# Gates of a graph network in pairs: half of the nodes as a difference on top of the other half's sums, and four relation products beside the gates

## The chip, the cores and the metric

The kernel runs on one core of a Trainium2 chip, as one launch. It is measured in device microseconds from the start to the end of an execution; the time before is the median of three runs, 1405.69 us (1404.71 to 1413.34). Five engines work side by side, each through its own queue in order: TensorE (PE, with its weight loads as PEld), VectorE (DVE), ScalarE (ACT), GpSimd (POOL) and SyncE (SP), which here only issues DMAs. They wait for each other by semaphores.

## The reference

The whole program is a stack of four graph layers, each followed by a feed-forward layer, on 256 nodes of 768 features. The change is in the first graph layer alone. It computes two rounds of this (x is 256 x 768; a batch of 8 graphs has 32 nodes each; 64 query vectors per graph):

```python
def _rgcn(x, W_rel, W_root, bias, src, dst, etype):
    xr = jnp.einsum('ni,rio->rno', x, W_rel)          # 3 relations
    msg = xr[etype, src]
    out = x @ W_root + bias
    for r in range(NUM_RELATIONS):
        m = etype == r
        s = segment_sum(where(m[:, None], msg, 0.0), dst)
        c = segment_sum(m, dst)
        out = out + s / jnp.maximum(c, 1.0)[:, None]
    return out

def _gate(h, q, Wg, bg, Wq, bq):
    h3 = h.reshape(B, N, F)
    hg = jnp.einsum('bnf,gf->bng', h3, Wg[:, :F])
    qg = jnp.einsum('blf,gf->blg', q, Wg[:, F:]) + bg
    attn = jax.nn.sigmoid(hg[:, :, None, :] + qg[:, None, :, :])
    qi = jnp.einsum('bnlf,blf->bnf', attn, q)
    alpha = jax.nn.sigmoid(h3 @ Wq[:, :F].T + qi @ Wq[:, F:].T + bq)
    return alpha * jnp.tanh(qi) + (1.0 - alpha) * h3

h = relu(_rgcn(x, W_rel1, W_root1, b1, ...)); h = _gate(h, ...)
h = relu(_rgcn(h, W_rel2, W_root2, b2, ...)); h = _gate(h, ...)
```

The costly part is `attn`: for every graph, node, query and feature one sigmoid of a sum of a node's term (hg) and a query's term (qg), multiplied by q and summed over the queries.

## The kernel before

The nodes are held in two chunks of 128 (four graphs each), the features as six blocks of 128 on the partitions. A round ("layer" in the loop at the end of the code) has these stages.

*Relation products and RGCN.* `z_of` (L457 to L466) multiplies one chunk of nodes with half of one relation's weights: six matmuls of 128x384. There are 12 such products in a round (3 relations, 2 chunks, 2 halves). The RGCN then adds, for each feature block, the root product and the relation products spread over the edges (`ps_rgcn`, L102 and L728); ScalarE's Relu gives `gT`.

*Terms.* `q_terms` and `node_terms` compute qg and hg, six matmuls for a half. `split3` takes each result apart into three bf16 parts that add up to it (ScalarE and VectorE in turn, over seven steps), and DMAs place the parts on partitions: `ga` holds the first two parts of the query terms, `gb` the third part and, on partitions 64 to 111, the three parts of 16 node terms. `gb` has two copies, u = 0 and 1, one for each half of a graph's 32 nodes. Most node rows go through a DRAM tile (`hg_rows`).

*Gates.* A unit is one graph and one feature block: 48 units a round. `form` (L758 to L771) makes a unit in two steps, u = 0 and 1. In each, TensorE sums the terms of 16 nodes with all 64 queries into two PSUM banks by multiplying with matrices of ones and zeros (`sela`, `selb`): two matmuls of 128x512 for each bank, four in all. Then ScalarE takes the sigmoid of the two banks at once (L769). A round thus has 384 gate matmuls. The bank pairs (`acc2`) are two in number. Of every three units, two are multiplied by q on GpSimd (L789) and one on VectorE (L796, for which ScalarE first copies q to the PSUM bank `qy`, L786); VectorE sums all (L774, `total`) into `qiT`. Gate tiles come from five buffers (tag `z`), which the relation products' results use as well.

*Beside the gates.* After each step's matmuls, `next(beside)` issues one further matmul of a chain of generators: the remaining `q_terms` and `node_terms`, then for each chunk the two halves of alpha's product (`alpha_nodes` L632, `alpha_gates` L647, the latter waiting until its sums are five steps old), and the first chunk's `blend`. Their follow-up work is put down by `later(n, ...)` to be issued n steps on. `blend` copies alpha from PSUM, transposes it, takes the sigmoid and a tanh (into bank `qy`), and mixes the new features `nT` on VectorE, in three turns whose distance is `gap` steps.

*End of a round.* What is left of the chain is issued, then the second chunk's `blend`. In the first round its turns alternate with the 12 relation products for the second round (`more`), in the second round with nothing.

The order on the engines is that of the program for everything inside `pin`; the rest, DMAs among it, is put in order by the framework. Each engine works strictly in its own order. Weights come through a ring of eight buffers, and a load is issued by SyncE when the buffer it replaces has had its last reader; `parts` tiles (`stg`) are three.

## Time and profile before

| what | us |
|---|---|
| median of three runs | 1405.69 |
| the profiled execution | 1404.96 |
| its span, first to last instruction | 1403.2 |
| first round: gates on TensorE | 134.3 to 284.3 |
| first round: gates on VectorE (first to last sum) | 144.2 to 297.7 |
| first round: last alpha, blend, 12 relation products | 297.7 to 348.0 |
| second round: RGCN | 348.0 to 379.1 |
| second round: gates on TensorE | 390.7 to 538.2 |
| second round: gates on VectorE (first to last sum) | 400.8 to 550.4 |
| second round: last alpha, blend | 550.4 to 559.7 |

The rest of the program, before 94 us and after 560 us, is not touched. Times in the profile are those of one execution; "busy" is the time in which an engine's instructions run. Matmuls overlap, so that the duration of one (379 ns for 128x512) is longer than the distance from one to the next (217 ns): sums of work on TensorE are made with the distance. An f32 matmul of 128x384 appears as two records, together 0.65 us. The number in brackets behind a row of a time line is the engine's idle time before it, with what ended that time.

### The profile page before, as it was taken

How to read it: one execution, taken by the hardware profiler on the slowest of the kernel's cores; microseconds unless marked ns; L12 is line 12 of the kernel's file. 1: busy time of each engine (PE TensorE's matmuls, PEld its weight loads, DVE VectorE, ACT ScalarE, POOL GpSimd, SP SyncE). 2: the span in 40 equal slices, each digit the busy share in tenths (PEclk: the TensorE clock that was granted, in tenths of full speed). 3: DMA queues.
4: the chain of work that ended last, by engine and by line, in shares of the span. 5: the costliest groups of instructions: out<-in, count | busy, mean ns of one | idle time of the engine just before them, and what ended most of it. 6: DMA issues, size and time to landing. Idle time of an engine off the chain costs nothing. (4 is left out here: it accounts for less than half of the span.)

```text
span 1403.2 us, 13971 instructions
## 1 busy us (share of the span) xinstructions
PE 1246.0 (89%) x5088; PEld 765.4 (55%) x5088; DVE 671.2 (48%) x1278; ACT 476.0 (34%) x826; POOL 360.1 (26%) x200
## 2 busy tenths in 40 slices
PE   7999999969998884799899978987887999878998
PEld 4576444436843442575545554545575545467854
DVE  4330899950069998406446271067252101365033
ACT  1012777721177764115114212215221111173122
POOL 1000999920069995000111101021011000100000
PEclk9999999989999997799999979998989999975989
DMA  9332150314240021241573139942019799801000
GB/s 343 124 110 96 45 180 19 102 34 167 104 127 8 0 102 44 76 166 40 195 293 117 53 125 363 364 170 102 23 59 347 286 392 402 344 1 36 32 0 23
DMA packets 77450, 196.92 MB, mean 140 GB/s; under 512 B 8764, under 2 KB 23712, under 8 KB 77248
## 3 DMA queue, kind: packets, MB, share of 16 engines
q1 hardware_dynamic: 69088, 162.28, 32.3%
q0 software_dynamic: 6576, 28.95, 5.8%
q10 hardware_dynamic: 1712, 4.72, 0.9%
q8 instruction: 44, 0.72, 0.2%
q14 instruction: 30, 0.25, 0.1%
HBM read 177.61 MB, written 14.87 MB: 137 GB/s over the span
## 5 line engine op out<-in xcount | busy, mean ns | idle before, releaser
L789 POOL TENSOR_TENSOR gate<-gate,qT 128x2048 f32<-128x2048 f32 x64 | 287.8, 4522 | 241.7 <-ACT gate L769 241.3
L774 DVE TENSOR_REDUCE qiT<-gate 128x32 f32<-128x2048 f32 x96 | 215.0, 2279 | 16.2 <-POOL gate L789 15.2
L769 ACT ACTIVATE gate<-gate_acc,bg 128x1024 f32<-128x1024 f32 x192 | 209.6, 1113 | 38.2 <-PE gate_acc L765 35.5
L764 PE MATMUL gate_acc<-sela,ga 128*128 128x512 bf16 x384 | 147.3, 384 | 25.2 <-ACT gate L769 24.5
L765 PE MATMUL gate_acc<-selb,gb 112*128 112x512 bf16 x384 | 147.8, 385 | 0.0
L1159 PE MATMUL up_acc<-w_e,xgT 128*64 128x384 f32 (+1 forms) x432 | 96.4, 489 | 0.0
L765 PEld LDWEIGHTS <-gb 112*128 112x128 bf16 x384 | 37.6, 98 | 96.2 <-issue 71.4
L796 DVE TENSOR_TENSOR gate<-gate,ps_qy 128x2048 f32<-128x2048 f32 x32 | 72.9, 2277 | 0.2 <-ACT gate L769 0.2
L1159 PEld LDWEIGHTS up_acc<-w_e,xgT 128*64 128x64 f32 (+1 forms) x432 | 46.9, 154 | 44.6 <-issue 27.2
L764 PEld LDWEIGHTS <-ga 128*128 128x128 bf16 x384 | 37.8, 98 | 47.7 <-issue 2.2
L647 PE MATMUL ps_alpha<-w_qb,qiT 128*128 128x384 f32 x96 | 44.1, 553 | 19.8 <-DVE qiT L774 19.8
L571 DVE TENSOR_TENSOR ps_hg<-ps_hg,hg 128x384 f32<-128x384 f32 x8 | 4.5, 562 | 107.8 <-ACT hg L570 107.8
L267 DVE CUSTOM_DVE_ANT_0 gat_dot<-xl,row 128x128 f32<-128x128 f32 (+2 forms) x56 | 23.8, 424 | 51.3 <-ACT xl L1537 18.9
L462 PE MATMUL ps_z<-w_rel,xT 128*128 128x384 f32 x144 | 47.9, 486 | 0.0
L462 PE MATMUL ps_z<-w_rel,nT 128*128 128x384 f32 x144 | 47.5, 490 | 0.0
L1126 POOL DMA_INDIRECT yg<-ys,rows x8 | 7.6, 953 | 153.5 <-DMA w_qk<-in_L_ffn_W_qkvT 100.9
L466 ACT COPY z<-ps_z 128x384 f32<-128x384 f32 x24 | 11.5, 478 | 104.5 <-PE ps_z L462 104.5
L1689 DVE TENSOR_TENSOR h<-up_acc,h 128x768 f32<-128x768 f32 x6 | 5.7, 957 | 80.1 <-PE up_acc L1159 80.1
L102 PE MATMUL ps_e<-xT,w_s 128*128 128x256 f32 x144 | 36.2, 417 | 7.4 <-DVE heads L1568 7.4
L171 PE MATMUL ps_tr<-ident,xn 128*128 128x128 f32 x84 | 16.7, 363 | 28.9 <-DVE xn L160 14.0
L632 PE MATMUL ps_alpha<-w_qa,gT 128*128 128x384 f32 x96 | 40.0, 498 | 0.0
L1126 POOL DMA_INDIRECT xg<-table,slots x12 | 11.7, 977 | 105.2 <-PE ps_xg L1134 46.3
(446 smaller groups left out, 2187.8 us busy)
## 6 DMA issues: line engine op xcount, KB each, us to landing
w_e<-in_L_ffn_W SPq DMA_DIRECT2D x32, 1152.0 KB, 12.2
w_rel<-in_L_gnn_W_rel SPq DMA_DIRECT2D x12, 1152.0 KB, 8.7
wi<-in_L_ffn_WiT SPq DMA_DIRECT2D x8, 1152.0 KB, 12.0
wo<-in_L_ffn_WoT SPq DMA_DIRECT2D x8, 1152.0 KB, 12.7
w_down<-in_L_ffn_W SPq DMA_DIRECT2D x8, 1152.0 KB
w_s<-in_L_ffn_Ws SPq DMA_DIRECT2D x5, 1152.0 KB, 8.9
w_root<-in_L_gnn_W_root SPq DMA_DIRECT2D x4, 1152.0 KB, 5.4
w_ga<-in_L_gnn_WgAT SPq DMA_DIRECT2D x4, 1152.0 KB
```

The source lines that it names most:

```text
L102: mm = nc.tensor.matmul(ps, w(k, lo, lo + P), xT[:, k, :], start=start and k == 0, stop=stop and k == kcs - 1)
L267: pin(nc.vector.tensor_tensor_reduce(t, xl[:, c, h * C:(h + 1) * C], r[:, h * C:(h + 1) * C], 1.0, 0.0, OP.mult, OP.add, accum_out=a2[:, w ...
L462: mm = nc.tensor.matmul(ps, hT[:, k, c * P:(c + 1) * P], w(k, i * 384, (i + 1) * 384), start=k == 0, stop=k == KD - 1)
L632: pin(nc.tensor.matmul(al_ps[c][i], hT[:, k, c * P:(c + 1) * P], w(k, i * 384, (i + 1) * 384), start=k == 0, stop=False))
L647: pin(nc.tensor.matmul(al_ps[c][i], qiT[:, f, c * P:(c + 1) * P], w(f, i * 384, (i + 1) * 384), start=False, stop=f == KD - 1))
L764: pin(nc.tensor.matmul(acc[:, i, :], ga[:, b, fs], sela, start=True, stop=False))
L765: pin(nc.tensor.matmul(acc[:, i, :], gb[0:112, u, b, fs], selb[0:112, i], start=False, stop=True))
L769: pin(nc.scalar.activation(g[:, u * 16:(u + 1) * 16, :].rearrange("p n l -> p (n l)"), acc.rearrange("p a n -> p (a n)"), AF.Sigmoid, bias ...
L774: pin(nc.vector.tensor_reduce(qiT[:, f, b * NPB:(b + 1) * NPB], g, AX.X, OP.add))
L789: pin(nc.gpsimd.tensor_tensor(g, g, q[:, None, :].to_broadcast([P, NPB, LQ]), OP.mult))
L796: pin(nc.vector.tensor_tensor(g, g, q_ps[:, None, :].to_broadcast([P, NPB, LQ]), OP.mult))
L1159: pin(nc.tensor.matmul(ps[at:at + n, :], xT[:, k, at:at + n], ws[r](k, lo, hi), start=start, stop=stop))
```

## The change

*Differences.* A graph's second 16 nodes are no longer summed anew. `step_nodes` writes, beside the first 16 nodes' features, the difference of the second 16 and the first 16 (into `d0` for the first chunk and into a free half of `nT` for the second), so that `node_terms` gives the terms of the first 16 nodes and differences of terms. The parts of the differences go to a new tile `gd`, by DMA from `hg_rows`, also for graph 0; `gb` has one copy and is loaded once. In `form` the second step (u = 1) adds, with one matmul of 48 rows for each bank and `start=False`, the differences to the sums that are still in the bank from the first step: two matmuls in place of four.

*Pairs.* `form` takes two units at once: first half of A, first half of B, second half of A, second half of B, in the two bank pairs. The copies of q for VectorE's units are issued ahead of the pair. In the first round the second halves issue two matmuls of the chain beside them, the others one as before.

*Relation products.* In the first round, four of the six products of the first chunk for the next RGCN (`z_beside`, relations 0 and 1) stand in the chain, between parts of the second chunk's `alpha_gates`; they use PSUM bank `sd`, and their results lie in the half of `qiT` that the first chunk no longer needs and in a new tile `z0`. One more is issued right after the last gates. The other seven follow the second chunk's blend, whose three turns now come at one step (`gap` 0). The first chunk's blend in the first round has gap 4 in place of 9.

```diff
-        gb = gt.tile([P, 2, NB, D], BF16, name="gb")
+        gb = gt.tile([P, NB, D], BF16, name="gb")
+        gd = gt.tile([P, NB // 2, D], BF16, name="gd")
...
+        seld = gt.tile([64, 2, 8, LQ], BF16, name="seld")
...
-                    for u in range(2):
-                        nc.sync.dma_start(gb[0:64, u, b, fs], parts[r, 2, :])
+                    nc.sync.dma_start(gb[0:64, b, fs], parts[r, 2, :])
...
+        def step_nodes(to, hT, c, o):
+            a, b = (t.rearrange("p (b u n) -> p b u n", b=4, u=2) for t in (hT[:, o, c * P:(c + 1) * P], to[:, o, :]))
+            nc.vector.tensor_copy(b[:, :, 0, :], a[:, :, 0, :])
+            nc.vector.tensor_tensor(b[:, :, 1, :], a[:, :, 1, :], a[:, :, 0, :], OP.subtract)
...
-                for u in range(2):
+                for s in range(3):
+                    nc.sync.dma_start(gb[64 + s * 16:80 + s * 16, c * 4 + j0:(c + 1) * 4, fs], v[0, s][:, j0:, :])
+                for o in range(2):
                     for s in range(3):
-                        nc.sync.dma_start(gb[64 + s * 16:80 + s * 16, u, c * 4 + j0:(c + 1) * 4, fs], v[u, s][:, j0:, :])
+                        nc.sync.dma_start(gd[o * 64 + s * 16:o * 64 + 16 + s * 16, c * 2:(c + 1) * 2, fs], v[1, s][:, o::2, :])
...
+        def z_beside(w, hT, z, c, i):
+            ps = one_bank("sd", "ps_z")[:, :384]
+            for k in range(KD):
+                pin(nc.tensor.matmul(ps, hT[:, k, c * P:(c + 1) * P], w(k, i * 384, (i + 1) * 384),
+                                     start=k == 0, stop=k == KD - 1))
+                if k == KD - 1:
+                    later(1, lambda: pin(nc.scalar.copy(z[:, i * 3:(i + 1) * 3, :],
+                                                        ps.rearrange("p (o n) -> p o n", o=3))))
+                yield
...
-            first, gap = (3, 9) if c == 0 else (2, 1)
+            first, gap = (3, 4 if layer == 0 else 9) if c == 0 else (2, 0)
...
-                                 lambda: pause(3), lambda: alpha_nodes(wa, gT, 1), lambda: alpha_gates(wb, qiT, 1))
+                                 lambda: pause(3), lambda: alpha_nodes(wa, gT, 1), lambda: after_blend(),
+                                 lambda: z_beside(ws[0], nT, zs0[0], 0, 0), lambda: alpha_gates(wb, qiT, 1, 0, 1),
+                                 lambda: z_beside(ws[0], nT, zs0[0], 0, 1), lambda: alpha_gates(wb, qiT, 1, 1, 2),
+                                 lambda: z_beside(ws[1], nT, zs0[1], 0, 0), lambda: alpha_gates(wb, qiT, 1, 2, 3),
+                                 lambda: z_beside(ws[1], nT, zs0[1], 0, 1), lambda: alpha_gates(wb, qiT, 1, 3))
...
-            def form(b, f):
-                fs = slice(f * P, (f + 1) * P)
-                g = wtile("gate", (NPB, LQ))
+            def form(pair):
+                gs = [wtile("gate", (NPB, LQ)) for _ in pair]
+                accs = [acc2("gate_acc") for _ in pair]
                 for u in range(2):
-                    acc = acc2("gate_acc")
-                    for i in range(2):
-                        pin(nc.tensor.matmul(acc[:, i, :], ga[:, b, fs], sela, start=True, stop=False))
-                        pin(nc.tensor.matmul(acc[:, i, :], gb[0:112, u, b, fs], selb[0:112, i], start=False, stop=True))
-                    steps[0] += 1
-                    next(beside, None)
-                    flush()
+                    for (b, f), g, acc in zip(pair, gs, accs):
+                        fs = slice(f * P, (f + 1) * P)
+                        h = slice(b % 2 * 64, b % 2 * 64 + 48)
+                        for i in range(2):
+                            if u == 0:
+                                pin(nc.tensor.matmul(acc[:, i, :], ga[:, b, fs], sela, start=True, stop=False))
+                                pin(nc.tensor.matmul(acc[:, i, :], gb[0:112, b, fs], selb[0:112, i],
+                                                     start=False, stop=True))
+                            else:
+                                pin(nc.tensor.matmul(acc[:, i, :], gd[h, b // 2, fs],
+                                                     seld[0:48, i] if b % 2 == 0 else selb[64:112, i],
+                                                     start=False, stop=True, skip_group_check=True))
+                        steps[0] += 1
+                        next(beside, None)
+                        if layer == 0 and u == 1:
+                            next(beside, None)
+                        flush()
...
-                if n % 3 == 2:
-                    at = (n // 3) % 4 * LQ
-                    q_ps = qy[:, at:at + LQ]
-                    pin(nc.scalar.copy(q_ps, q))
-                g = form(b, f)
+                if n % 2 == 0:
+                    for m in range(n, n + 2):
+                        if m % 3 == 2:
+                            at = (m // 3) % 4 * LQ
+                            q_ps = qy[:, at:at + LQ]
+                            bm, fm = units[m]
+                            pin(nc.scalar.copy(q_ps, qT[:, fm, bm * LQ:(bm + 1) * LQ]))
+                    pair = form(units[n:n + 2])
+                g = pair[n % 2]
...
+            if layer == 0:
+                zs = [wtile("z", (NC, D)) for _ in range(NREL)]
+                more = [(r, c, i) for c in range(NC) for r in range(NREL) for i in range(2) if c or zs0[r] is None]
+                r, c, i = more.pop(0)
+                z_of(ws[r], hT, zs[r], c, i, True)
...
-                if more:
+                if more and not pending:
                     r, c, i = more.pop(0)
                     z_of(ws[r], hT, zs[r], c, i, True)
```

## The prediction

> **What bounds the kernel now.** I read the page's engine list first, then the time line of each engine in the two gate stages, then busy time by stretch. The page's chain of waits starts only at 1057 us, so it says nothing of the part that is changed; the time lines have to carry it.

> ```profile
> PE 1246.0 (89%) x5088; PEld 765.4 (55%) x5088; DVE 671.2 (48%) x1278; ACT 476.0 (34%) x826; POOL 360.1 (26%) x200
> ...
> L764 PE MATMUL gate_acc<-sela,ga 128*128 128x512 bf16 x384 | 147.3, 384 | 25.2 <-ACT gate L769 24.5
> L765 PE MATMUL gate_acc<-selb,gb 112*128 112x512 bf16 x384 | 147.8, 385 | 0.0
> ```

> TensorE is busy 89% of the span, and these two rows, 295 us of it, are what the change cuts. An average over stages, though. VectorE in the middle of the first gate stage:

> ```profile
> 226.45 6.67 DVE L774 TENSOR_REDUCE qiT<-gate 128x32 f32<-128x2048 f32 x3
> 233.04 2.28 DVE L796 TENSOR_TENSOR gate<-gate,ps_qy 128x2048 f32<-128x2048 f32 x1
> 235.35 6.67 DVE L774 TENSOR_REDUCE qiT<-gate 128x32 f32<-128x2048 f32 x3
> 241.94 2.28 DVE L796 TENSOR_TENSOR gate<-gate,ps_qy 128x2048 f32<-128x2048 f32 x1
> 244.25 6.67 DVE L774 TENSOR_REDUCE qiT<-gate 128x32 f32<-128x2048 f32 x3
> ```

> No row has an idle bracket. Three units cost 3 sums and 1 multiply, 8.90 us, so six cost 17.80. From 144.2 to 297.7 us VectorE pauses once, for 0.6 us. GpSimd is as full: in the second layer one row holds 22 products in 98.63 us, four (six units' worth) in 17.93. Busy time by stretch (columns: stretch, length, PE, PEld, DVE, ACT, POOL busy, granted TensorE clock, DMA):

> ```profile
> 190.00:242.00 52.00, 50.36 (x201) 24.94 (x199) 51.83 (x30) 39.62 (x45) 50.47 (x13) 1.00 0.27 77
> ...
> 284.00:300.00 16.00, 5.52 (x10) 2.52 (x9) 13.52 (x9) 2.74 (x4) 6.08 (x2) 0.62 0.00 0
> 300.00:348.00 48.00, 48.00 (x152) 28.32 (x151) 3.84 (x9) 8.41 (x21) 0.00 (x0) 0.99 0.37 125
> ...
> 440.00:500.00 60.00, 49.31 (x189) 22.21 (x188) 59.62 (x30) 42.05 (x49) 60.00 (x15) 0.97 0.00 1
> ```

> The gate stages belong to VectorE and GpSimd; TensorE only keeps up. At 284 it has run out of work and waits for the last sums; from 300 to 348 it alone works, on relation products:

> ```profile
> 297.74 2.93 PE L647 MATMUL ps_alpha<-w_qb,qiT 128*128 128x384 f32 x4 [5.97 <-DVE qiT L774]
> 300.46 4.48 PE L462 MATMUL ps_z<-w_rel,nT 128*128 128x384 f32 x12
> ...
> 313.18 35.00 PE L462 MATMUL ps_z<-w_rel,nT 128*128 128x384 f32 x108
> ```

> **The change, part by part.** The base is the profiled execution's own 1404.96 us (span 1403.2), 0.7 below the median of the runs.

> *Fewer gate matmuls.* A unit falls from 8 to 6 of 128x512. They start 0.217 us apart, so TensorE loses 96 x 2 x 0.217 = 41.7 us of work. Both gate stages are paced by others: this saves nothing by itself. It makes room.

> *Moved products.* A relation product is 3.87 us (35.00 us for nine). By the program's order four of the first chunk's six stand between gates, the fifth behind the last gate, where TensorE idles 4.5 and 6.0 us, and the sixth stays after the blend. Before, the last sum ends at 297.69 and the second layer's first product starts at 348.01: 50.3 us. Afterwards: the last alpha matmuls and the blend's transposes, 4.1 us by the same steps in the second layer (550.43 to 554.53), then seven products, 27.1, and 0.3 for a slow first one. The blend ends 9.3 us after the last sum (559.71 there), the sixth product covers it until 8.2, and the next needs the last two of its features only 2.6 us later. So 31.5: **18.8 us saved**. The loads of the second W_root and of W_ga leave on the same releases, earlier with them.

> *Start of a stage.* The first unit is now whole after three sigmoids, not two: +1.1 (L769's 1.113 us) per layer, since VectorE idles 7.5 us for GpSimd there: **+2.2**.

> *Steady state.* The second half's matmuls wait for the sigmoid on the same bank; the beside products and the next pair queue behind them on TensorE. They are two (0.43 us) and run beside the other unit's sigmoid. More delicate is the copy of q (L786): it waits for VectorE's multiply three units back, because both use the bank qy, and for an odd unit it now stands ahead of both units' sigmoids. Take that multiply's end as 0: copy 0.2, three sigmoids 3.15, so the pair's first product can start at 3.35; GpSimd's previous one ends at 3.5. The next pair can have its sigmoids from 4.4, its product from 7.6; GpSimd wants it at 8.0. VectorE needs the results at 11.1 and 13.3, they are there at 8.0 and 12.5. I take 0 extra, with margins of 0.15 and 0.4 us.

> *Clock.* Row first: after idle times of 4.5 and 6.0 us, two 128x384 products took 2.72 us, not 1.3, at a granted clock of 0.62. [...] In the second layer a unit's gates become 6 x 0.217 = 1.3 us in 2.97. [...]

> *Blend of the first chunk, gap 9 to 4.* Its tanh writes bank qy, so it too queues behind VectorE's use of it, and VectorE's steps wait in turn. Following the order: the first step finds VectorE done with a sum at 2.2 and tanh behind copy, two alpha copies (0.85), two sigmoids and itself at 3.7: 1.5 lost; second and third steps wait for tanh after the previous mix, 0.45 each; the last mix waits for one sigmoid and two of 0.35, 1.4; GpSimd, held by the same sigmoids, then makes VectorE wait 0.75. Total 4.6, before 0.6: **+4.0** (bounds 1 to 5.5, since ScalarE may run ahead more than I assume). In the second layer gap 9 stays; before it lost 2.0, I find about the same, **+0.5** (-1 to 3).

> *Last pairs.* With six beside steps of 0.65 a pair costs TensorE 2.6 + 3.9 = 6.5 us, VectorE 5.94. Over 4.3 pairs 2.4 us, mostly taken up by the lead: **+0.7** (0 to 2.4). The products share one bank (sd); their copy stands behind one sigmoid and is done before the next begins.

> *Copies, DMAs.* Per layer 24 small VectorE steps form the differences (64 elements each); a row of 256 elements (L868) takes 0.28 us, so 24 are under 6.7 us, VectorE idles 33 and 68 us there, and the last one has five matmuls (3.2 us) before it is needed: 0 (to 1). SyncE issues 10 instead of 7 loads for a second-chunk node half and 6 instead of 8 for a query half, at 0.5 to 0.6 us each; the second-half rows of graph 0 now come through DRAM too. They leave at about 133.5 to 135, land 1.9 later, and are wanted at 138.5 after the first sigmoid (137.4): 0 (to 3). In the pair of units 10 and 11 the cast of a query half waits for loads queued behind two w_rel loads of 5.9 us: **+0.5** (0 to 4).

> Sum: -18.8 + 2.2 + 4.0 + 0.5 + 0.7 + 0.5 = -10.9: **1394 us**.

> **Rivals.** *Waits mostly hidden.* ScalarE waits 19 and 16 us for gate matmuls in the two stages, so it may be further ahead than I assume; then the blend costs 1 and the rest nothing: 1404.96 - 18.8 + 2.2 + 1 = 1389.4. *Beside work crowds out the gain.* If lead is short, the last pairs lose their 2.4, the DMA wait its 4, the second blend 3 and the first 5.5: 1404.96 - 18.8 + 2.2 + 14.9 = 1403. *TensorE is the bound after all* (89%, 50.36 of 52 us): then all of 41.7 comes off too, 1344; against it, a VectorE without gaps. *Slower: the copy of q starves GpSimd.* If the path from multiply to product is 1.7 us longer than 3.35 (a slow clock and slower handovers), GpSimd idles 1.55 us every six units; 16 such groups give 25: 1394 + 25 = 1419, and at 2.5 us, 1434. It turns the gain to a loss from 0.15 + 10.9/16 = 0.8 us of lateness. For it: margins of 0.15 and 0.4; against it, only VectorE's last sum counts and GpSimd's lead of 0.8 absorbs the first group.

> **How the numbers follow.** A measurement tells about 1% from no change. Forecast 0.53 (1391 to 1399); hidden waits 0.22 (1389); crowding 0.14 (1403); starved GpSimd 0.07 (1419 and up); TensorE bound 0.04 (1344). 1% is 1390.9: faster takes the hidden waits, the TensorE case and the forecast's lower edge, 0.30; slower the starved case and a little of crowding, 0.09; the rest, 0.61, within 1%. The range 1387 to 1406 leaves out the last two cases and little else.

> **What would show it.** L764 and its partners down from 768 matmuls to 576, VectorE still without idle brackets between gates at 17.8 to 18 us for six units, first VectorE sum 1.1 us later; idle brackets of 0.5 to 1.5 us at the blend lines; from the last sum to the second layer's L102 31.5 us instead of 50.3; the second layer's stage within 2 us of its 149.7. Repeated idle of GpSimd for the gate sigmoid, once every six units, would make it wrong, as would a VectorE that runs faster than before.

## The result and the profile after

The changed kernel takes 1423.78 us (median of nine, 1421.64 to 1427.63) against 1405.69 before (nine runs too, 1404.44 to 1417.03): ratio 1.0112, 95% interval 1.0089 to 1.0136. It is slower by 18 us by the medians, 16 by the ratio; 11 us of gain were forecast, and the range of 1387 to 1406 misses it. The profiled execution has a span of 1422.7 us, 19.5 more than before. By stretch (in us, read off the time lines of both kernels):

| stretch | before | after | difference | forecast |
|---|---|---|---|---|
| start to first VectorE sum, first round | 144.2 | 145.0 | +0.9 | +1.1 |
| first gate stage, first to last sum | 153.5 | 175.0 | **+21.5** | +5.2 |
| last sum to the second round's first L102 | 50.3 | 29.9 | **-20.4** | -18.8 |
| RGCN | 31.2 | 31.2 | 0 | 0 |
| to first sum of the second round | 21.5 | 23.2 | +1.7 | +1.1 |
| second gate stage | 149.7 | 154.7 | **+5.1** | +0.5 |
| last blend (9.3 us), then to the first branch of the program's rest | 293.1 | 294.2 | +1.1 | 0 |
| first to second branch | 211.6 | 221.5 | **+9.9** | 0 |
| from there to the end | 348.1 | 347.9 | -0.2 | 0 |

The moved products did what was said, and a little more. Two gate stages gave it back, and 10 us were lost 280 us behind the last line that the diff touches. First the busy time by stretch of the changed kernel (stretch, length, PE, PEld, DVE, ACT, POOL busy, granted clock, DMA):

```profile
190.00:242.00 52.00, 42.13 (x128) 16.70 (x128) 44.20 (x23) 32.65 (x38) 42.46 (x11) 0.87 0.15 53
284.00:320.00 36.00, 36.00 (x121) 16.98 (x120) 33.49 (x16) 21.21 (x25) 29.06 (x7) 1.00 0.10 33
320.00:350.00 30.00, 29.91 (x97) 17.48 (x96) 3.92 (x10) 6.61 (x17) 0.00 (x0) 1.00 0.57 200
440.00:500.00 60.00, 45.62 (x147) 16.81 (x147) 57.75 (x27) 43.78 (x49) 58.43 (x14) 0.86 0.00 0
```

In the stretch where VectorE had been busy 51.83 of 52 us it is now busy 44.20, and so is GpSimd: 7.6 us of idle time on the engine that sets the pace. TensorE does less there (42.13 against 50.36 us) and at a lower granted clock (0.87 against 1.00). From 284 to the last sum at 320 TensorE is full. The waits of the first stage (what waits for what, us in all, times, longest), after:

```profile
ACT ps_qy L839 <- DVE gate L850: 17.1, 7, 4.2
PE gate_acc L811 <- ACT gate L819: 12.9, 10, 4.1
...
DVE qiT L824 <- POOL gate L843: 9.4, 5, 4.2
ACT qg L575 <- PE ps_qg L587: 9.4, 4, 2.4
```

The first row does not exist before in this stage: ScalarE's copy of q (L839) waits seven times for VectorE's multiply, and a chain follows, TensorE for ScalarE, VectorE for GpSimd. In the second round the copy waited before the change too, and the wait doubles; before and after:

```profile
ACT ps_qy L786 <- DVE gate L796: 10.7, 9, 2.1
...
ACT ps_qy L839 <- DVE gate L850: 22.2, 8, 3.9
```

The last row of the first stage is another thing: ScalarE, ahead of its work, waits for TensorE to finish a query term. TensorE in the first 40 us of the stage, the first matmul of each pair:

```profile
142.37 0.38 PE L807 MATMUL gate_acc<-sela,ga 128*128 128x512 bf16 x1
...
149.72 0.38 PE L807 MATMUL gate_acc<-sela,ga 128*128 128x512 bf16 x1
...
157.07 0.38 PE L807 MATMUL gate_acc<-sela,ga 128*128 128x512 bf16 x1
...
164.38 0.38 PE L807 MATMUL gate_acc<-sela,ga 128*128 128x512 bf16 x1
```

No row has an idle bracket, and a pair takes 7.35 us. GpSimd, which needs 5.98 for a pair's share (four products of 4.48 per three pairs), shows it in the same stretch:

```profile
151.54 9.02 POOL L843 TENSOR_TENSOR gate<-gate,qT 128x2048 f32<-128x2048 f32 x2 [2.05 <-ACT gate L819]
162.26 9.00 POOL L843 TENSOR_TENSOR gate<-gate,qT 128x2048 f32<-128x2048 f32 x2 [1.71 <-ACT gate L819]
173.50 4.52 POOL L843 TENSOR_TENSOR gate<-gate,qT 128x2048 f32<-128x2048 f32 x1 [2.24 <-ACT gate L819]
```

So TensorE paces the start of the stage. After 12 sums VectorE is 11.7 us later than before. The end of the stage, on TensorE:

```profile
313.41 4.03 PE L462 MATMUL ps_z<-w_rel,nT 128*128 128x384 f32 x12
...
317.92 4.03 PE L670 MATMUL ps_alpha<-w_qb,qiT 128*128 128x384 f32 x12
...
322.91 27.26 PE L462 MATMUL ps_z<-w_rel,nT 128*128 128x384 f32 x84
350.00 2.32 PE L102 MATMUL ps_rgcn<-nT,w_root 128*128 128x256 f32 x10
```

One product stands behind the last gates, seven (84 records, 27.26 us) behind the blend's transposes, as counted in the forecast.

Last, what lies behind the gates. At the first branch (before: L1453, after: L1510) TensorE and VectorE idle (in the kernel before 1.36 and 1.34 us, ended by the branch's line). The next TensorE row, before:

```profile
844.98 0.59 PE L1389 MATMUL ps_cw<-ident,router_l 128*8 128x128 f32 x2 [1.36 <-PEq L1453]
```

and after:

```profile
860.63 0.58 PE L1446 MATMUL ps_cw<-ident,router_l 128*8 128x128 f32 x2 [7.15 <-issue]
```

"issue" means that it waited for nothing that the profile shows. TensorE stood 5.8 us longer in code that is the same. The other 4.1 of the 9.9 us up to the second branch come in three steps of 1.0 to 1.7 us further on; no run took them apart.

### The profile page after: what moved, and what is told of

Same layout as the page of the kernel before. It is cut to its first block, busy times and chain, and to the rows that moved or that the text cites. A ratio compares the mean times of both kernels' runs of the same rounds, so it can differ in the third digit from the quotient of the medians.

```text
span 1422.7 us, 13634 instructions
## 1 busy us (share of the span) xinstructions
PE 1251.2 (88%) x4896; PEld 746.2 (52%) x4896; DVE 682.3 (48%) x1330; ACT 474.4 (33%) x826; POOL 360.3 (25%) x200
## 5 line engine op out<-in xcount | busy, mean ns | idle before, releaser
L824 DVE TENSOR_REDUCE qiT<-gate 128x32 f32<-128x2048 f32 x96 | 215.9, 2281 | 14.4 <-POOL gate L843 13.3
L807 PE MATMUL gate_acc<-sela,ga 128*128 128x512 bf16 x192 | 80.7, 420 | 10.4 <-ACT gate L819 9.9
L808 PE MATMUL gate_acc<-selb,gb 112*128 112x512 bf16 x192 | 81.2, 423 | 0.0
L811 PEld LDWEIGHTS <-gd 48*128 48x128 bf16 x192 | 13.2, 96 | 87.9 <-issue 87.2
L811 PE MATMUL gate_acc<-seld,gd 48*128 48x512 bf16 x96 | 31.4, 409 | 23.0 <-ACT gate L819 22.9
L462 PE MATMUL ps_z<-w_rel,xT 128*128 128x384 f32 x144 | 47.9, 486 | 0.0
L1183 POOL DMA_INDIRECT yg<-ys,rows x8 | 7.7, 956 | 154.8 <-DMA w_qk<-in_L_ffn_W_qkvT 101.3
L644 PE MATMUL ps_alpha<-w_qa,gT 128*128 128x384 f32 x96 | 45.0, 568 | 0.0
L811 PE MATMUL gate_acc<-selb,gd 48*128 48x512 bf16 x96 | 32.9, 426 | 12.4 <-ACT gate L819 12.3
L808 PEld LDWEIGHTS <-gb 112*128 112x128 bf16 x192 | 20.1, 105 | 43.8 <-issue 33.7
L102 PE MATMUL ps_e<-xT,w_s 128*128 128x256 f32 x144 | 36.8, 422 | 7.0 <-DVE heads L1625 7.0
L171 PE MATMUL ps_tr<-ident,xn 128*128 128x128 f32 x84 | 17.4, 375 | 28.3 <-DVE xn L160 13.3
```

The lines of the kernel that those rows point to most:

```text
L102: mm = nc.tensor.matmul(ps, w(k, lo, lo + P), xT[:, k, :], start=start and k == 0, stop=stop and k == kcs - 1)
L462: mm = nc.tensor.matmul(ps, hT[:, k, c * P:(c + 1) * P], w(k, i * 384, (i + 1) * 384), start=k == 0, stop=k == KD - 1)
L644: pin(nc.tensor.matmul(al_ps[c][i], hT[:, k, c * P:(c + 1) * P], w(k, i * 384, (i + 1) * 384), start=k == 0, stop=False))
L807: pin(nc.tensor.matmul(acc[:, i, :], ga[:, b, fs], sela, start=True, stop=False))
L808: pin(nc.tensor.matmul(acc[:, i, :], gb[0:112, b, fs], selb[0:112, i], start=False, stop=True))
L811: pin(nc.tensor.matmul(acc[:, i, :], gd[h, b // 2, fs], seld[0:48, i] if b % 2 == 0 else selb[64:112, i], start=False, stop=True, skip_gro ...
```

## The experiments

Twelve kernels ran. Times are medians; ratios are against the kernel before on the same chip; stages and tail (last sum to L102) are from each run's profile; the last column is TensorE's idle time at the first branch, us.

| kernel | us | ratio (95%) | stage 1 | tail | stage 2 | branch |
|---|---|---|---|---|---|---|
| before | 1405.7 | | 153.5 | 50.3 | 149.7 | 1.36 |
| changed | 1423.8 | 1.0112 (1.0089 to 1.0136) | 175.0 | 29.9 | 154.7 | 7.15 |
| changed, pad | 1415.6 | 1.0050 (1.0035 to 1.0066) | 173.1 | 29.9 | 154.8 | 1.23 |
| before, pad | 1415.7 | 1.0055 (1.0042 to 1.0069) | 153.9 | 51.3 | 148.5 | 7.14 |
| changed, pad in bank sd | 1417.6 | 1.0066 (1.0046 to 1.0085) | 175.5 | 29.9 | 154.7 | 1.33 |
| pairs alone | 1442.9 | 1.0237 (1.0195 to 1.0280) | 168.4 | 50.3 | 156.8 | 7.04 |
| pairs alone, late copy | 1428.1 | 1.0140 (1.0123 to 1.0157) | 159.2 | 50.4 | 153.5 | 7.12 |
| pairs of eight, late copy | 1421.5 | 1.0090 (1.0060 to 1.0119) | 157.3 | 51.0 | 151.4 | 1.33 |
| changed, late copy | 1428.0 | 1.0135 (1.0094 to 1.0176) | 182.5 | 29.7 | 150.9 | 7.08 |
| the same once more | 1426.4 | 1.0133 (1.0115 to 1.0151) | 182.3 | 29.7 | 150.9 | 7.14 |
| changed, slow start | 1422.1 | 1.0107 (1.0065 to 1.0149) | 167.9 | 30.6 | 156.7 | 7.06 |
| slow start, late copy | 1408.1 | 1.0009 (0.9995 to 1.0024) | 161.2 | 29.7 | 150.6 | 7.12 |
| slow start, late copy, pad | 1400.7 | 0.9958 (0.9942 to 0.9974) | 161.8 | 29.7 | 150.9 | 1.33 |
| before, three products moved | 1393.6 | 0.9907 (0.9890 to 0.9924) | 153.5 | 38.3 | 148.6 | 1.34 |

Each stage is read from one profiled execution. The same code differs from kernel to kernel: the changed kernel's first stage takes 173.1 to 175.5 us in its three rows without other edits, the second stage of the kernel before 148.5 to 149.7, that of pairs with the late copy 150.6 to 153.5. Differences of 2 to 3 us between two rows therefore show nothing by themselves.

Three theories stood at the start: that the branch's stall comes from where it lies in TensorE's instruction stream; that six beside matmuls a pair make TensorE the bound; that the copy of q starves GpSimd, which was the prediction's fourth rival.

### The branch: 64 idle matmuls at the start

```diff
     nc.vector.memset(eps_t, EPS)
+    few = const.tile([P, 8], BF16, name="few")
+    nc.vector.memset(few, 0.0)
+    ps = bank("ps_few")
+    for _ in range(64):
+        nc.tensor.matmul(ps[:8, :8], few, few, start=True, stop=True)
```

> The changed kernel with 64 more 8x8 TensorE matmuls (128 instructions with their weight loads, of data nobody reads) in the first 9.7 us, in which TensorE waits for the first norm anyway. The change takes 192 gate matmuls, 384 instructions, out of TensorE's stream, which shifts all that follows by 384, or by 128 within blocks of 256, the size in which the trace's instruction transfers (16 KB each) come. Theory A (after the second gate stage 5.8 of the lost us come from where the first branch falls in those blocks: TensorE idled 7.15 us after it, before the change 1.36): the pad puts the branch back to the place it had, the idle falls to about 1.4 us, the time to 1418. Theory B (the idle comes from loads that are shifted in time): idle stays at about 7 us, 1424.

> The kernel before with the same 64 small matmuls at its start. Theory A: the branch now falls where the changed kernel has it, TensorE idles about 7 us after it instead of 1.36, and the time rises by 5 to 6 us to 1411. Theory B: nothing changes, 1405.7, idle 1.4.

Both came out as theory A says: the pad takes the stall away from the changed kernel (7.15 to 1.23 us) and gives it to the kernel before (1.36 to 7.14):

```profile
861.24 0.59 PE L1394 MATMUL ps_cw<-ident,router_l 128*8 128x128 f32 x2 [7.14 <-issue]
```

The totals moved by more than 5.8 us (by the ratios, 8.7 down and 7.7 up). `bank` hands out PSUM banks in turn, so that the pad also turned the banks of all later code: the first router's matmuls took some 4 us longer, a part near the end some 5 less. The run was therefore repeated with a bank that leaves the turn alone:

```diff
-    ps = bank("ps_few")
+    ps = one_bank("sd", "ps_few")
```

> As the first pad on the changed kernel, but its 64 small matmuls write a bank with one buffer, so that the turn of the banks in the rest of the program stays as it was (the first pad turned it, and router matmuls far behind changed by 3.5 us). If the place of the branch in TensorE's stream is worth 5.8 us and nothing else is moved: 1418, idle after the branch 1.2 to 1.4 us, all stages as in the changed kernel. If the first pad's gain was the banks' turn: 1424.

1417.6 us and 1.33 us idle; stages and tail stay within 0.5 us of the changed kernel's. The ratio falls from 1.0112 to 1.0066, 6.5 us (each ratio is known to about 3 us): the 5.8 of the idle time and perhaps a little of the half clock behind it (granted clock from 854 to 867 us was 0.50 in the changed kernel, 0.74 from 844 to 857 us in the kernel before). The profiled executions differ by 5.8 us in span.

```profile
856.23 0.58 PE L1451 MATMUL ps_cw<-ident,router_l 128*8 128x128 f32 x2 [1.33 <-PEq L1515]
```

What goes with the stall can be read from the transfers of instructions (queue q8, 16 KB each; from 55.5 to 526.1 us of the kernel before 14 of them for 1659 matmuls and as many weight loads, 118 matmuls for one). In the 6 us ahead of the branch the kernel before has one; the changed kernel has none in the 15 us ahead of it, and its next falls inside the idle time. In the transfers of the changed kernel from 853.5 to 860.6 us, packets, MB and share:

```profile
DMA packets 1044, 2.80 MB, mean 394 GB/s; under 512 B 60, under 2 KB 512, under 8 KB 1042
...
q8 instruction: 1, 0.02, 0.9%
```

The profiles of all fourteen kernels agree in this. Where TensorE idles 1.2 to 1.4 us, the transfer begins 2.4 to 3.3 us ahead of the idle time; where it idles 7.0 to 7.2, the transfer begins some 4.4 us into it (at 857.94 us in the changed kernel, whose idle time is 853.48 to 860.63). The transfer itself takes 1.0 to 1.1 us in both cases. That TensorE waits there for its instructions is the author's estimate from these times: no view names what it waits for, and in the changed kernel its next matmul starts 1.6 us after the transfer's end (859.01). The price here is 5.8 us. Whether the branch itself was taken the profiles don't say (no instruction of its own block, L1454 to L1461, stands in the trace), and whether the DMA engines, full of expert weights at 394 GB/s, lengthen the idle time no run tested.

### The pairs alone

```diff
-            first, gap = (3, 4 if layer == 0 else 9) if c == 0 else (2, 0)
+            first, gap = (3, 9) if c == 0 else (2, 1)
...
-                        if layer == 0 and u == 1:
-                            next(beside, None)
...
-                                 lambda: z_beside(ws[0], nT, zs0[0], 0, 0), lambda: alpha_gates(wb, qiT, 1, 0, 1),
...
+                                 lambda: pause(3), lambda: alpha_nodes(wa, gT, 1), lambda: alpha_gates(wb, qiT, 1))
```

> Gates in pairs with the second half on top of the first, as in the changed kernel, but everything else as before: one beside step per half, gap 9, all twelve relation products after the gates. By the prediction's steps pairs cost 2.2 us at the starts and nothing else: 1408. Theory C (the copy of q ahead of both units of a pair and the lower clock cost what the second layer of the changed kernel shows, 5 us a stage, and the branch another 5.8): first stage 153.5 + 5 = 158.5 us, second 154.7, in all 1423. If the crowding of TensorE by six beside matmuls a pair is what costs 11.7 us in the first 12 units of the changed kernel, then here VectorE reaches its 12th sum within 3 us of before (183.2), not 11.7 later.

1442.9 us, the slowest of all: the first stage takes 14.9 us more than before, the second 7.1. The 12th sum is 4.5 us late, not 11.7; so most of the crowding is indeed the double beside step. But from then on the pairs lose time that the double beside step can't explain, as it is gone. One such place, in the time lines of all four engines:

```profile
158.06 13.48 POOL L836 TENSOR_TENSOR gate<-gate,qT 128x2048 f32<-128x2048 f32 x3 [0.55 <-ACT gate L812]
167.50 2.27 DVE L843 TENSOR_TENSOR gate<-gate,ps_qy 128x2048 f32<-128x2048 f32 x1
169.81 0.22 ACT L832 COPY ps_qy<-qT 128x64 f32<-128x64 f32 x1 [4.18 <-DVE gate L843]
171.12 0.59 PE L806 MATMUL gate_acc<-selb,gd 48*128 48x512 bf16 x2 [2.98 <-ACT gate L812]
173.16 4.53 POOL L836 TENSOR_TENSOR gate<-gate,qT 128x2048 f32<-128x2048 f32 x1 [1.62 <-ACT gate L812]
174.46 0.63 PE L802 MATMUL gate_acc<-sela,ga 128*128 128x512 bf16 x1
```

The copy waits 4.18 us until VectorE's multiply is through; the pair's sigmoids stand behind it, so TensorE waits 2.98 us for the bank, and GpSimd 1.62 for its product. In the last row a gate matmul takes 0.63 us instead of 0.38, because the granted clock has fallen to 0.50 meanwhile (from 173.0 us on).

### The copy behind the sigmoids

```diff
                 if n % 2 == 0:
-                    for m in range(n, n + 2):
-                        if m % 3 == 2:
...
-                            pin(nc.scalar.copy(q_ps, qT[:, fm, bm * LQ:(bm + 1) * LQ]))
                     pair = form(units[n:n + 2])
+                if n % 3 == 2:
+                    at = (n // 3) % 4 * LQ
+                    q_ps = qy[:, at:at + LQ]
+                    pin(nc.scalar.copy(q_ps, q))
```

> The changed kernel with the copy of q behind the pair's sigmoids, right ahead of the multiply that needs it, instead of ahead of the pair's matmuls. If the copy is what holds ScalarE (3.76 us at 195.6, 3.83 at 218.0, and the steps of 0.5 to 2 us of the second layer): the second stage falls from 154.7 to about 150, the first from 175 to about 168, in all 1412. If the sigmoids are late for another reason (the matmuls' own order, the clock): second stage 154 to 155, 1423.

> The pairs alone (previous run: 1443, stages of 168.4 and 156.8 us instead of 153.5 and 149.7) with the copy of q behind the pair's sigmoids. If the copy ahead of both units is what costs the pairs their time (there it waited 4.18 us for VectorE's multiply every six units, TensorE idled 2.98 us behind it and then ran at half clock): first stage about 157, second about 151, in all 1426. If the second half's wait for its own unit's sigmoid, or the lower clock as such, is the cause: stages as before the edit, 1443.

In the second round the expectation held in the changed kernel: 154.7 to 150.9. With the pairs alone the stages fell by 9.2 and 3.3 us, to 159.2 and 153.5 (157 and 151 were expected), and the total to 1428.1 (1426 was expected). But the changed kernel's first stage got *longer*, 175.0 to 182.5, against the expected 168. There TensorE makes the sigmoids late, and a copy behind them is late as well; VectorE's multiply, which in the changed kernel never waited for the copy, now does:

```profile
151.48 2.29 DVE L848 TENSOR_TENSOR gate<-gate,ps_qy 128x2048 f32<-128x2048 f32 x1 [4.61 <-ACT ps_qy L838]
```

So the copy and the crowding are not independent, and the crowding had to be taken away first.

### The slow start

```diff
-                        if layer == 0 and u == 1:
+                        if layer == 0 and u == 1 and steps[0] - first_step > 56:
                             next(beside, None)
```

> The changed kernel with the late copy of q, and with two beside steps per second half only from step 57 on (when the node, query and first alpha matmuls are through); before that one, as in the kernel before. If six beside matmuls a pair make TensorE the bound (7.33 us a pair against 5.93 to 7 of VectorE): the 12th sum comes 3 to 5 us later than before, not 11.7 (17.8 with the late copy alone), the first stage takes about 162 instead of 182, the tail 34 to 38, in all 1413. If not: first stage 175 to 182, 1424 to 1428.

This first attempt tested `steps[0] > 56`, but the counter goes up by 100 in each earlier `run`, so it was always above; the kernel was the late copy once more, and its 1426.4 tells how well such a run repeats (1428.0). With the counter's value at the first unit subtracted (`first_step`), with and without the late copy:

> The changed kernel with the late copy of q, and now truly with two beside steps per second half only after the first 56 halves of the first stage (the run before counted from a step counter that already stood far above 56, so its condition was always true and it repeated the late copy alone). If six beside matmuls a pair make TensorE the bound early in the stage: the 12th sum comes 3 to 5 us later than before, not 17.7; blend and last pairs cost about 9 as in the changed kernel, first stage about 167, tail 30 to 36, in all 1416. If not: 1426 to 1428.

> The same slow start with the copy of q where the changed kernel has it, ahead of both units. If crowding and copy add up: the 12th sum 4.5 us later than before, first stage about 168. If the copy's wait takes the place of the crowding once TensorE has room (as in the pairs alone, where units 16 to 26 lost 6 us): 12th sum 4.5 us later, but the first stage back at 173 to 178, 1422 to 1428.

With the copy where it was, the 12th sum is 4.9 us late instead of 11.7 and the first stage takes 167.9 instead of 175.0, so crowding is worth 7.2 us there, and the copy does not take it back. The total, though, is 1422.1, only 1.7 us less, which the other theory had named: in code that is the same, the second stage took 2.0 us longer than in the changed kernel and the way from there to the first branch some 3. With the late copy the 12th sum is 5.4 late (of which 3.2 come from a later first sum), the stages take 161.2 and 150.6, and the total is 1408.1, 8 us better than I expected. From one to the other the copy alone is worth 6.7 and 6.2 us of stage and 14 us in all, give or take 6 by the intervals. The second stage's figure is 3.8 between the changed kernel with and without the late copy, and 3.3 between the pairs alone; in the five rows of six matmuls with the early copy this stage takes 154.7 to 156.8 us, in the five with the late copy 150.6 to 153.5.

The first stage's 21.5 us are thus 7.2 for crowding, 6.7 for the copy, and 7.7 that stay in the slow start with late copy: 2.2 by the 12th sum, 3.8 at the blend and 2.1 in the last eight sums, less 0.3 between. Taken in the other order the split is another (the late copy first costs 7.5, the slow start then saves 21.3); the sum of both, 13.8, does not depend on the order.

### Pairs with eight matmuls a unit

```diff
+                    if u == 1:
+                        accs = [acc2("gate_acc") for _ in pair]
...
-                                pin(nc.tensor.matmul(acc[:, i, :], gd[h, b // 2, fs],
...
+                            pin(nc.tensor.matmul(acc[:, i, :], ga[:, b, fs], sela, start=True, stop=False))
+                            pin(nc.tensor.matmul(acc[:, i, :], gb[0:112, b, fs], selb[0:112, i],
+                                                 start=False, stop=True))
```

> The pairs alone with the late copy, but each second half formed anew with the four matmuls of the first half, on a bank of its own: eight matmuls a unit as before, in the order of pairs. The second 16 nodes take the first ones' rows, so the differences are left out of the result; the work on all engines is that of before. If the work taken off TensorE is what lets its clock fall and makes the sigmoids late: half-clock time in the stages falls to what it was before (0 and 28 us up to the last sums), first stage 155, second 151, and with 384 more instructions the branch stands where it stood before, 1412. If the order of the pairs is what costs: stages 159 and 153.5 as with six matmuls, and 1420 from the branch alone.

Busy time in the second stage, six matmuls a unit:

```profile
400.00:563.00 163.00, 130.21 (x394) 48.48 (x394) 147.12 (x77) 109.82 (x125) 144.15 (x34) 0.83 0.14 48
```

and eight:

```profile
399.00:560.00 161.00, 127.86 (x481) 58.57 (x490) 146.79 (x77) 109.66 (x125) 144.21 (x34) 0.95 0.15 48
```

With a quarter fewer gate matmuls TensorE is no less busy, because its clock is 0.83 instead of 0.95. (Some matmul records of the second run are missing, 481 for 490 weight loads, so that its 127.86 is up to 3 us too low.) The traces of the kernel before and the changed one have a granted clock of 1.00 or 0.50 and nothing between; so a mean of 0.83 over 163 us is 55 us at half clock, 0.95 over 161 is 16. In these two runs, then, the work taken off TensorE lowered its clock.

That this costs time is not shown. The stages are 1.9 and 2.0 us shorter with eight matmuls than with six (157.3 and 151.4 instead of 159.2 and 153.5), but the second stage of the slow start with late copy has the same instructions as that of the pairs alone with late copy, six matmuls a unit, and it takes 150.6 us at a clock of 0.86:

```profile
383.00:543.00 160.00, 123.37 (x387) 46.94 (x394) 146.93 (x77) 109.07 (x125) 144.10 (x34) 0.86 0.15 49
```

The changed kernel with the late copy (twice) and the slow start with late copy and pad take 150.9, at 0.81 to 0.82 from the first to the last sum. None of them is slower than eight matmuls at 0.95. In the first stage the difference lies in the last eight sums (30.1 us with six, 27.9 with eight), and the pairs alone with the early copy, six matmuls too, pass these in 27.6. The clock is worth between 0 and 2 us a stage, and the runs don't narrow that down.

What stays is 3.7 us in the first stage against the kernel before (157.3 to 153.5) and 1.7 to 2.9 in the second: the price of the pairs, by their order or by the differences' own steps and loads, which I did not take apart further. The branch's idle time is 1.33 us here, with 384 instructions more. The total, 1421.5, was nevertheless at the 1420 of the other theory, since some 7 us more than before lie between the last sum and the second branch, in code that is the same; I did not follow them further.

### What beats the kernel before

```diff
+            if layer == 0:
+                zs = [wtile("z", (NC, D)) for _ in range(NREL)]
+                more = [(r, c, i) for c in range(NC) for r in range(NREL) for i in range(2)]
+                r, c, i = more.pop(0)
+                z_of(ws[r], hT, zs[r], c, i, True, one_bank("sd", "ps_z")[:, :384])
             for _ in beside:
...
+            if layer == 0:
+                for _ in range(2):
+                    r, c, i = more.pop(0)
+                    z_of(ws[r], hT, zs[r], c, i, True)
+                for _ in alpha_gates(wb, qiT, 1, 5):
...
```

(`alpha_gates` takes a range of blocks here, and `z_of` a bank to write to.)

> The kernel before, gates unpaired and gap 9; only three of the first chunk's relation products are moved: one behind the last gate matmul, two behind the next alpha pair, in the 4.5 and 6.0 us in which TensorE idles for the last sums. If idle TensorE time there is free: about 9 us of products go in, the next 3.7 us at half clock go too, the tail from last sum to the second layer's first product falls from 50.3 to 40, in all 1396. If the moved products hold up the last alpha matmuls or wait for banks and buffers: 1402 to 1406.

1393.6 us, ratio 0.9907: more than expected. TensorE at the end of the first stage and behind it:

```profile
286.23 4.14 PE L463 MATMUL ps_z<-w_rel,nT 128*128 128x384 f32 x12 [1.85 <-DVE ps_qy L686]
290.21 1.45 PE L648 MATMUL ps_alpha<-w_qb,qiT 128*128 128x384 f32 x4
291.50 7.90 PE L463 MATMUL ps_z<-w_rel,nT 128*128 128x384 f32 x24
299.24 1.45 PE L648 MATMUL ps_alpha<-w_qb,qiT 128*128 128x384 f32 x4
...
336.02 2.75 PE L102 MATMUL ps_rgcn<-nT,w_root 128*128 128x256 f32 x12
```

The alpha pair that took 2.93 us before, at a granted clock of 0.50 (287.69 to 301.34 us), takes 1.45. The last sum is where it was (297.73), the tail 38.3 instead of 50.3. The last pair of alpha starts 1.5 us later than before, and nine products still follow on TensorE, so that the later start costs nothing there.

> The changed kernel with the three costs that the runs found taken off together: slow start of the beside steps, copy of q behind the pair's sigmoids, and the 64 small matmuls at the start that put the branch back to its old place. If the three are separate costs, the time of the first two edits (1408.1) falls by the branch's 5.8: 1402, the first stage 161, the second 150.5, idle after the branch 1.3; 0.3 to 0.5% under the kernel before. If the branch's stall only moves elsewhere: 1408.

The changed kernel with its three costs off takes 1400.7 us, 0.4% under the kernel before: once crowding and copy are gone, the branch's cost comes off as a third (7.4 us, 5.8 of them the idle time). It has the shorter tail of the two, but its gate stage is still 8 us longer, so that three moved products alone, with no pairs and no differences, do better.

## Why the prediction was wrong

**What bounds the kernel.** Right for the kernel before; but the reading "TensorE only keeps up" was carried over to a changed kernel with six beside matmuls a pair, where it does not.

**Moved products, -18.8.** Right: -20.4, with seven products in 27.26 us behind the transposes.

**Start of a stage, +2.2.** About right: +0.9 and +1.7.

**Steady state, 0.** Wrong, and this is the step with the largest share: GpSimd was held to have its lead at every pair. The path was right: copy, three sigmoids, first product 3.35 us after the multiply's end. In the pairs alone the multiply ended at 169.77 and the product began at 173.16, 3.4 us. What failed is the other end of the margin: "GpSimd's previous one ends at 3.5". There it ended at 171.54, 1.8 us after the multiply's end. In the first round VectorE also has the split steps (0.56 us each; four of them stand between 160.03 and 163.11 in that run), which delay its multiply against GpSimd; I had costed them for nobody. In the second round of the changed kernel, with hardly any of them, the margin of 0.15 was too small all the same. GpSimd, in the first half of that stage:

```profile
418.24 18.03 POOL L843 TENSOR_TENSOR gate<-gate,qT 128x2048 f32<-128x2048 f32 x4 [0.99 <-ACT gate L819]
437.48 17.93 POOL L843 TENSOR_TENSOR gate<-gate,qT 128x2048 f32<-128x2048 f32 x4 [1.21 <-ACT gate L819]
455.87 17.95 POOL L843 TENSOR_TENSOR gate<-gate,qT 128x2048 f32<-128x2048 f32 x4 [0.46 <-ACT gate L819]
```

That is a wait for the sigmoid once every six units, the sign that the prediction had named. The copy cost 6.7 us in the first stage and 3.3 to 6.2 in the second. It was the fourth rival, with its place (odd units, copy ahead of both), and it got 0.07 because GpSimd's lead was to absorb the first group and only VectorE's last sum to count; its own trace of the kernel before had the copy waiting 10.7 us in the second stage. That the measured 1423.8 lies where this rival put it (1419 and up) is in part luck: the rival had the copy alone cost 25 us, and it cost some 10 in the stages; crowding and the branch made up the rest.

**Last pairs, +0.7.** The price was named and the place was not, which is the second step that failed. Six beside matmuls were counted at 6.5 us a pair against VectorE's 5.94, but only for the last 4.3 pairs. The program issues two per second half in the whole round, so the first seven pairs carry the 42 matmuls of the terms in the same density, and there a pair takes 7.35 us. That cost 7.2 us by the slow start. Of the 0.85 above 6.5, changes between gate and f32 matmuls are not the cause: in the kernel before, they follow each other at 0.87 for four gate matmuls and 0.65 for an f32 one (205.13, 206.00, 206.65 us). In the changed kernel two f32 ones beside a half of 48 rows take 1.49 (146.31 to 147.80), where 1.30 were counted; why, no run shows. The last pairs themselves cost 2.1 us in the slow start with late copy, inside the bound of 2.4.

**Blend with gap 4, +4.0.** Right: from the 30th to the 40th sum 3.8 us in the slow start with late copy. In the second round +0.5 was forecast, and the whole stage is 0.9 longer in that run.

**Clock, no term in the sum.** Open between 0 and about 2 us a stage. The granted clock was 0.84 in the changed kernel's second stage (394 to 559 us), 0.93 before (390 to 551). At half clock the gate matmuls start 0.43 us apart (206.97, 207.39 and 207.82 us in the changed kernel) instead of 0.217, so that a unit's six take an estimated 2.6 us of its 2.97. That this is enough holds in the second round as far as the runs show: six matmuls at 0.81 to 0.86 took no longer than eight at 0.95. The estimate is for a TensorE with time to spare. In the changed kernel's first stage half clock also fell where TensorE had none, right behind the waits for the copy (from 201.92 us, after 1.70 us of idle time up to 200.63), so that a part of the copy's price there may be the clock's.

**Cast behind DMAs, +0.5.** One wait of 3.3 us for a DMA out of the same buffer is there in the first stage (bound 4), against one of 2.3 at such a place before the change; no run separated it.

**Everything behind the changed part, tacitly 0.** Wrong by 10.8 us in the profile, of which the place of the branch is 5.8 and, in measured totals with the clock behind it, 6.5. "Saves nothing by itself" was said of the 192 matmuls taken out; taking out instructions also moves all later ones. The rest, about 5 us, stays open.

Together: -20.4 of gain, 26.6 in the two stages (forecast 5.7), 2.6 at their starts and 10.8 behind, +19.6.

## What to carry to other kernels

When a change makes two units share what one had (a copy ahead of both, a bank for both), margins have to be worked out with everything that the engines do in that stretch, the side work included, and a margin of a few tenths of a microsecond is no margin. Work moved beside other work is to be counted in every stretch where the new density holds, not only in the one it was made for. If the aim is to fill an engine's idle time, look first at whether the idle time can take the work as it is: three products in 10 us of TensorE idle gave more than the whole rebuilt stage.
